# A hybrid layer stack on one core: ternary quantisation of the feed-forward weights moved beside the gated memory

## The chip, the cores and the metric

The kernel runs on one core of one Trainium2 chip. A core has five instruction queues that work beside each other and wait for each other through semaphores: TensorE (PE, matmuls), VectorE (DVE), ScalarE (ACT), GpSimd (POOL) and SyncE (SP, which here issues every DMA). The metric is the device time of the program in microseconds (us), as the median over runs. One execution was profiled; its trace gives a start and a duration for each instruction.

## The reference

Four sub-layers follow one another on a residual stream of 2048 tokens (2 sequences of 1024) by 512 features: a gated linear memory, a feed-forward, a differential attention, and the same feed-forward again with the same weights. Each takes a layer norm of the stream.

```python
x = x + gated_memory(layernorm(x), w_in, w_out)
x = x + ffn(layernorm(x), w_gate_up, w_proj)
x = x + differential_attention(layernorm(x), ...)
x = x + ffn(layernorm(x), w_gate_up, w_proj)
```

The gated memory projects to q, k, v, a, g, and per channel runs a recurrence in chunks of 64 tokens: `prefix = cumprod(a)`, `acc = cumsum(k*v / max(prefix, 1e-6))`, `states = prefix * (state + acc)`, then `y = gate*(q*states) + (1-gate)*v` and a last projection. The feed-forward is `rms_norm(silu(gate) * up) @ w_proj`, and both its weight matrices are first made ternary:

```python
w = w_fp32.astype(bfloat16); w_g = w.reshape(-1, 64)
scale = clip(mean(abs(w_g), axis=-1, keepdims=True), 1e-8, None)
q = clip(round(w_g / scale), -1, 1)
w_hat = (q * scale).reshape(w.shape)
return w + stop_gradient(w_hat - w)
```

So each group of 64 weights becomes -scale, 0 or +scale, and the difference to w is rounded once in bf16 before w is added back.

## The kernel before

**Stage A, the gated memory** (lines 138 to 289). The 2048 tokens are 4 blocks of 512 (`t`), and the 512 channels are 4 chunks of 128 (`c`), channels on the partitions and tokens along the free dimension. Per block, PE first makes the q projections, then for each chunk the k, v, a and g projections (`kv`, `ag`, in a PSUM pool of two slots) and a broadcast of the q norms (`pr`, in a PSUM pool of four banks). ACT evicts these with tanh, sigmoid or copy. DVE and POOL then pass one 128x512 chunk to and fro, in this order:

- POOL: `u*v` (L232)
- DVE: clip of a (L233), `qn` (L273), `a_start`, memset, the scan for `prefix` (L239), its maximum and reciprocal `inv` (L242, L243)
- POOL: `u*inv` (L244)
- DVE: the scan for `acc` (L246), the scan over chunk states (L253), `acc+state` (L262)
- POOL: `acc*prefix` (L268); DVE: `acc*qn` (L274); POOL: `acc-v` (L275); DVE: `acc*gate` (L276); POOL: `yt = acc+v` (L277)

When the four chunks of a block are in `yt`, PE projects them (`a_out`, L284: 4 tiles of 128 tokens by 4 chunks of channels, so 16 matmuls, each of which is recorded as two passes) and DVE adds them to the residual `xres` (L289). The next block's layer norm and transposes (`xn`, `xnt`, in `a_input`) are issued before that projection, and the q projections of the next block after it.

**The feed-forward** (L336 on) is called twice. A block of 512 tokens goes through 16 chunks `f` of the hidden dimension: gate and up projections (L370), `silu(gate)*up` split into a high and a low part `hs` on ACT and DVE (L375 to L379), the down projection into four PSUM banks (L391), one chunk behind. `finish_block` takes the mean square (`msq`), a square root on ACT (`inv`, L404) and adds to the residual (L408). The weights of all 16 chunks stay in SBUF as tiles `ws[f]` of 128 by 3 by 512 (gate, up, down), in pools that lie where those of stage A were.

In the first call (`with_quant`) the ternary weights are made during the first block of 512 tokens: `ternary_chunk(f+1)` is issued ahead of the matmuls of chunk f. `ternary` works on one 128x512 tile: a DMA, three ACT passes (bf16 copy, magnitude, sign), a matmul with `groupmean` that leaves each group's mean in all of its rows, and on DVE the eviction of the scale (L309), the comparison (L312), the products with sign and scale (L313, L314) and the difference to w (L316); POOL adds w (L318) and ACT casts into `ws[f]` (L319). Three tiles make a chunk, which is also written to a DRAM tile `w_kept[f]` (L329). The second call loads `ws[f]` from there (L418).

**What sets the order.** The text of the program is traced once, a scheduler places the instructions of each engine in one fixed list, and each engine works through its list in order. An instruction whose inputs are late holds up all behind it on its engine. Tile pools with two buffers make the writer of a tile wait for the readers of the tile two before.

Of the kernel before, what the change touches and what calls it, by code (L numbers as in the profile page):

```python
# [10 lines left out]
F32 = mybir.dt.float32  # L11
F32R = mybir.dt.float32r
# [5 lines left out]
P = 128  # L18
# [24 lines left out]
def kernel(  # L43
# [91 lines left out]
        return pt.rearrange("p (c t) -> p c t", c=NKC)  # L135


    with ExitStack() as s:
        open_psum(s, "a")
        wa = s.enter_context(tc.tile_pool(name="wa", bufs=1))  # L140
        ap_ = s.enter_context(tc.tile_pool(name="a_act", bufs=2))

        w_sec = []
        for i in range(5):
# [54 lines left out]
        for t in range(NBLK):  # L199

            q = ap_.tile([P, NKC, BLK], F32, tag="q", name=f"q{t}", bufs=1)
            pss = bank(f"pss{t}")
            for c in range(NKC):
                pq = bank(f"pq{t}_{c}")
                project(pq, w_q, c, xt)
                nc.scalar.copy(q[:, c, :], pq)
                sq = ap_.tile([P, BLK], F32, tag="sq", name=f"sq{t}_{c}")
                nc.scalar.square(sq, pq)
                nc.tensor.matmul(
                    pss[:16, :], headmean[:, c, :], sq, start=(c == 0), stop=(c == NKC - 1)  # L210
                )
            rq = ap_.tile([16, BLK], F32, tag="rq", name=f"rq{t}")
            nc.scalar.activation(rq, pss[:16, :], AF.Sqrt, bias=rms_eps[:16])
            nc.vector.reciprocal(rq, rq)

            yt = ap_.tile([P, NKC, BLK], F32, tag="yt", name=f"yt{t}", bufs=1)
            for c in range(NKC):
                n = f"{t}_{c}"
                kv, ag = big(f"kv{n}"), big(f"ag{n}")
                project(kv[:, 0, :], w_k, c, xt)  # L220
                project(kv[:, 1, :], w_v, c, xt)
                project(ag[:, 0, :], w_a, c, xt)
                project(ag[:, 1, :], w_g, c, xt)
                u = ap_.tile([P, BLK], F32, tag="u", name=f"u{n}")
                nc.scalar.activation(u, kv[:, 0, :], AF.Tanh)
                v = ap_.tile([P, BLK], F32, tag="v", name=f"v{n}")
                nc.scalar.copy(v, kv[:, 1, :])
                a = ap_.tile([P, BLK], F32, tag="a", name=f"a{n}")
                nc.scalar.activation(a, ag[:, 0, :], AF.Sigmoid, bias=two)
                gate = ap_.tile([P, BLK], F32, tag="gate", name=f"gate{n}")  # L230
                nc.scalar.activation(gate, ag[:, 1, :], AF.Sigmoid)
                nc.gpsimd.tensor_mul(u, u, v)  # L232
                nc.vector.tensor_scalar(a, a, A_MIN, A_MAX, ALU.max, ALU.min)  # L233

                start = a_start[c % 2]
                nc.vector.tensor_copy(start[:, 0:BLK:CHUNK], a[:, 0:BLK:CHUNK])
                nc.vector.memset(a[:, 0:BLK:CHUNK], 0.0)
                prefix = ap_.tile([P, BLK], F32, tag="prefix", name=f"prefix{n}")
                nc.vector.tensor_tensor_scan(prefix, a, start, 0.0, ALU.mult, ALU.add)  # L239

                inv = ap_.tile([P, BLK], F32, tag="inv", name=f"inv{n}")
                nc.vector.tensor_scalar(inv, prefix, PREFIX_MIN, None, ALU.max)  # L242
                nc.vector.reciprocal(inv, inv)  # L243
                nc.gpsimd.tensor_mul(u, u, inv)  # L244
                acc = ap_.tile([P, BLK], F32, tag="acc", name=f"acc{n}")
                nc.vector.tensor_tensor_scan(acc, goes_on, u, 0.0, ALU.mult, ALU.add)  # L246

                state = ap_.tile([P, CPB + 1], F32, tag=f"state{c}", name=f"state{n}")
                if t % (SEQ // BLK) == 0:
                    nc.vector.memset(state[:, 0:1], 0.0)  # L250
                else:
                    nc.vector.tensor_copy(state[:, 0:1], before[c][:, CPB : CPB + 1])
                nc.vector.tensor_tensor_scan(  # L253
                    state[:, 1 : CPB + 1],
                    acc[:, CHUNK - 1 : BLK : CHUNK],
                    prefix[:, CHUNK - 1 : BLK : CHUNK],
                    state[:, 0:1],
                    ALU.add,
                    ALU.mult,
                )  # L260
                before[c] = state
                nc.vector.tensor_tensor(  # L262
                    acc.rearrange("p (n i) -> p n i", i=CHUNK),
                    acc.rearrange("p (n i) -> p n i", i=CHUNK),
                    state[:, 0:CPB].unsqueeze(2).to_broadcast([P, CPB, CHUNK]),
                    ALU.add,
                )
                nc.gpsimd.tensor_mul(acc, acc, prefix)  # L268

                pr = bank(f"pr{n}")  # L270
                nc.tensor.matmul(pr, headrow[:, c, :], rq, start=True, stop=True)
                qn = ap_.tile([P, BLK], F32, tag="qn", name=f"qn{n}")
                nc.vector.tensor_mul(qn, pr, q[:, c, :])  # L273
                nc.vector.tensor_mul(acc, acc, qn)  # L274
                nc.gpsimd.tensor_sub(acc, acc, v)  # L275
                nc.vector.tensor_mul(acc, acc, gate)  # L276
                nc.gpsimd.tensor_add(yt[:, c, :], acc, v)  # L277

            if t + 1 < NBLK:
                xt = a_input(t + 1)  # L280
            for j in range(TPB):
                po = bank(f"a_out{t}_{j}")
                for k in range(NKC):
                    nc.tensor.matmul(  # L284
                        po, yt[:, k, ts(j, P)], w_out[:, k, :],
                        start=(k == 0), stop=(k == NKC - 1),
                    )
                xi = xres[t * TPB + j]
                nc.vector.tensor_add(xi, xi, po)  # L289

    kept = ctx.enter_context(tc.tile_pool(name="kept", bufs=1, space=bass.MemoryType.DRAM))
    w_kept = [kept.tile([P, 3, D], F32R, tag=f"wk{f}", name=f"w_kept{f}") for f in range(NF)]

    def ternary(pool, dst, src, name):

        w32 = pool.tile([P, D], F32, tag="w32", name=f"w32_{name}", bufs=3)
        nc.sync.dma_start(out=w32, in_=src)
        w16 = pool.tile([P, D], BF, tag="w16", name=f"w16_{name}")  # L300
        nc.scalar.copy(w16, w32)
        mag = pool.tile([P, D], BF, tag="mag", name=f"mag_{name}")
        nc.scalar.activation(mag, w32, AF.Abs)
        sign = pool.tile([P, D], BF, tag="sign", name=f"sign_{name}")
        nc.scalar.sign(sign, w16)
        pm = ring(f"pm_{name}")
        nc.tensor.matmul(pm, groupmean, mag, start=True, stop=True)
        scale = pool.tile([P, D], BF, tag="scale", name=f"scale_{name}")
        nc.vector.tensor_scalar(scale, pm, SCALE_MIN, None, ALU.max)  # L309

        q = pool.tile([P, D], BF, tag="q", name=f"q_{name}")
        nc.vector.scalar_tensor_tensor(q, scale, TERNARY_CUT, mag, ALU.mult, ALU.is_lt)  # L312
        nc.vector.tensor_mul(q, q, sign)  # L313
        nc.vector.tensor_mul(q, q, scale)  # L314

        nc.vector.tensor_sub(q, q, w16)  # L316
        wq = pool.tile([P, D], BF, tag="wq", name=f"wq_{name}")
        nc.gpsimd.tensor_add(wq, q, w16)  # L318
        nc.scalar.copy(dst, wq)  # L319

    def ternary_chunk(pool, f, w):

        for e, src in enumerate((
            w_gu[f].rearrange("p c n -> p (c n)"),
            w_gu[NF + f].rearrange("p c n -> p (c n)"),
            w_pt[ts(f, P), :],
        )):
            ternary(pool, w[:, e, :], src, f"{'gud'[e]}{f}")
        nc.sync.dma_start(out=w_kept[f].bitcast(F32), in_=w.bitcast(F32))  # L329

    rings = []

    def ring(name):
        return rings[-1].tile([P, BLK], F32, tag="ring", name=name)

    def feed_forward(which, with_quant, store):  # L336
        with ExitStack() as s:
            wqp = s.enter_context(tc.tile_pool(name=f"wq{which}", bufs=1))
            ws = [wqp.tile([P, 3, D], F32R, tag=f"w{f}", name=f"w{which}_{f}") for f in range(NF)]
# [71 lines left out]
                    if store:  # L411
                        nc.sync.dma_start(out=out[ts(i, P), :], in_=xres[i])

            if with_quant:
                ternary_chunk(fp, 0, ws[0])
            else:
                for f in range(NF):
                    nc.sync.dma_start(out=ws[f].bitcast(F32), in_=w_kept[f].bitcast(F32))  # L418
            xs = ff_input(0)
            waiting = []  # L420

# [6 lines left out]
            for t in range(NBLK):  # L428
# [3 lines left out]
                    for j in range(TPB)  # L432
                ]
                for f in range(NF):
                    if with_quant and t == 0 and f + 1 < NF:
                        ternary_chunk(fp, f + 1, ws[f + 1])
                    hp = gate_up(t, f, xs, ssq)
                    if waiting:
                        down_one()
# [5 lines left out]
                down_one()  # L445
            rings.pop()

    feed_forward(0, True, False)


    NQ = SEQ // P
# [434 lines left out]
            for j in range(e * QB, (e + 1) * QB):  # L886
                project_out(1, j, w_o)

    feed_forward(1, False, True)


_INS = [
# [57 lines left out]
```

## Time and profile before

| what | value |
|---|---|
| time of the program, median of 3 runs | 2530.82 us (2530.42 to 2536.12) |
| profiled execution: its own time, and the span of its trace | 2533.64 us, 2531.9 us |
| stage A: until the last addition of `a_out` | 419.1 us, four blocks of some 100 us |
| first block of the first feed-forward, to its `inv` | 419.1 to 632.8 us |
| second block of it | 632.8 to 725.9 us |
| first block of the second feed-forward, to its `inv` | 2141.0 to 2253.3 us |
| busy over the span: PE, DVE, ACT, POOL | 94%, 44%, 36%, 16% |

The stage times are starts of instructions in the trace: the last L289 of stage A, the last attention addition before the second feed-forward, and the L404 that ends a feed-forward block. A busy share is an average over stages with different limits; what a change in one stage is worth is read in that stage, from the wait that ends last there. Starts and durations in the trace overlap a little: the next instruction of an engine begins some 0.1 us before the recorded end of the one before, so costs are best taken from start to start.

### The profile page before, as it was taken

The page shows a single profiled execution, that of the slowest core. Times are in us where ns is not written, and L with a number is a line of the kernel's source. Part 1 is how long each engine was busy: PE and PEld are TensorE (multiplying, and loading weights), DVE is VectorE, ACT ScalarE, POOL GpSimd, SP SyncE. Part 2 cuts the span into 40 slices and gives each one's busy share as a digit, 9 for nine tenths or more (in the row PEclk, how much of TensorE's full clock was granted, in tenths as well). Part 3 has the DMA queues.
Part 4 walks back from the last instruction along what each step waited for, and adds up shares of the span by engine and source line. Part 5 has one row for each costly group of instructions (what it writes and reads, how often), then busy time and mean ns, then how long its engine had stood idle before and what let it go on. Part 6 is the DMA issues. An engine that isn't in the chain of part 4 may idle for free. (4 is left out here: it accounts for less than half of the span.)

```text
span 2531.9 us, 26379 instructions
## 1 busy us (share of the span) xinstructions
PE 2382.2 (94%) x10050; PEld 1362.7 (54%) x10128; DVE 1109.4 (44%) x1551; ACT 885.7 (35%) x1340; POOL 403.0 (16%) x555
## 2 busy tenths in 40 slices
PE   8999996667999989999999999999999997999998
PEld 3443432445787854444545444444444543787887
DVE  4653647887323243343434343333434434423322
ACT  2122122767333321343434341233434440333333
POOL 1321312344221210000000000100000001122122
PEclk9999997889999999999999999999999998999999
DMA  4000001333000024342333331133333301300000
GB/s 166 0 1 0 0 0 46 125 110 119 1 1 1 1 80 108 83 97 76 90 88 85 81 90 52 51 81 97 76 102 82 78 12 65 137 17 1 17 17 17
DMA packets 66350, 148.84 MB, mean 59 GB/s; under 512 B 16048, under 2 KB 24240, under 8 KB 66224
## 3 DMA queue, kind: packets, MB, share of 16 engines
q1 hardware_dynamic: 66224, 147.15, 20.3%
q8 instruction: 80, 1.31, 0.2%
q14 instruction: 46, 0.38, 0.0%
HBM read 96.50 MB, written 41.94 MB: 55 GB/s over the span
## 5 line engine op out<-in xcount | busy, mean ns | idle before, releaser
L715 ACT ACTIVATE pr<-t 128x1024 f32<-128x1024 f32 (+3 forms) x384 | 311.0, 812 | 498.8 <-PE t L713 351.0
L659 DVE TENSOR_REDUCE nmax<-s 128x1 f32<-128x640 f32 (+3 forms) x256 | 259.3, 1023 | 270.7 <-PE s L651 270.4
L730 PE MATMUL y<-pr,val 128*33 128x512 f32 (+3 forms) x1536 | 325.6, 493 | 0.0
L391 PE MATMUL f_out<-w,hs 128*128 128x512 f32 x1024 | 274.3, 409 | 30.1 <-ACT hs L378 29.0
L370 PE MATMUL g<-xs,w 128*128 128x512 f32 x1024 | 275.2, 412 | 0.7 <-ACT xs L359 0.7
L370 PE MATMUL u<-xs,w 128*128 128x512 f32 x1024 | 261.8, 397 | 0.0
L647 PE MATMUL s<-ks,qs 128*128 128x512 f32 (+3 forms) x768 | 256.9, 408 | 3.2 <-ACT lam L562 0.5
L385 POOL TENSOR_TENSOR ssq<-ssq,sq 128x512 f32<-128x512 f32 x120 | 157.8, 1315 | 558.6 <-ACT sq L384 558.6
L376 DVE TENSOR_TENSOR h<-h,u 128x512 f32<-128x512 f32 x128 | 88.0, 687 | 359.8 <-PE u L370 354.6
L391 PEld LDWEIGHTS f_out<-w,hs 128*128 128x128 f32 x1024 | 196.7, 194 | 88.3 <-ACT hs L378 38.8
L370 PEld LDWEIGHTS g<-xs,w 128*128 128x128 f32 x1024 | 200.1, 196 | 70.8 <-issue 16.0
L703 PE MATMUL t<-qs,ks 128*128 128x512 f32 (+3 forms) x768 | 237.7, 391 | 0.0
L370 PEld LDWEIGHTS u<-xs,w 128*128 128x128 f32 x1024 | 193.9, 189 | 47.6 <-ACT w L319 0.2
L703 PEld LDWEIGHTS t<-qs,ks 128*128 128x128 f32 x768 | 117.3, 192 | 122.0 <-DVE nmax L659 45.0
L674 POOL CAST maxima<-nmax 128x8 bf16<-128x8 f32 x64 | 12.9, 201 | 1049.4 <-DVE nmax L659 684.4
L707 PE MATMUL t<-mt_s,pick 128*128 128x512 bf16 (+3 forms) x690 | 174.3, 325 | 5.3
L573 PE MATMUL pq<-b_xt,w_qk 128*128 128x512 f32 x384 | 170.2, 597 | 0.0
L655 DVE TENSOR_REDUCE nmax<-s 128x2 f32<-128x256 f32 (+3 forms) x128 | 104.7, 824 | 130.2 <-PE s L651 96.9
L647 PEld LDWEIGHTS s<-ks,qs 128*128 128x128 f32 x768 | 132.4, 192 | 50.0 <-ACT pr L715 22.4
L378 ACT CAST hs<-h 128x512 fp32r<-128x512 f32 x128 | 79.3, 619 | 216.9 <-DVE h L376 216.9
L730 PEld LDWEIGHTS y<-pr,val 128*33 128x33 f32 x1536 | 78.6, 110 | 124.6 <-issue 95.6
L375 ACT ACTIVATE h<-g 128x512 f32<-128x512 f32 x128 | 76.4, 597 | 189.1 <-PE g L370 189.0
(178 smaller groups left out, 2701.5 us busy)
## 6 DMA issues: line engine op xcount, KB each, us to landing
qs<-sc SPq DMA_DIRECT2D x128, 256.0 KB, 4.4
sc<-parts SPq DMA_DIRECT2D x192, 128.0 KB, 2.2
ks<-sc SPq DMA_DIRECT2D x128, 128.0 KB, 3.6
w_kept<-w SPq DMA_DIRECT2D x16, 768.0 KB, 3.5
w<-w_kept SPq DMA_DIRECT2D x16, 768.0 KB, 14.2
share<-ys SPq DMA_DIRECT2D x128, 64.0 KB, 2.0
w_in<-in_w_in_t_dram SPq DMA_DIRECT2D x5, 1024.0 KB, 10.8
x<-in_x_dram SPq DMA_DIRECT2D x16, 256.0 KB, 7.1
```

What stands on the lines that cost most here:

```text
L370: nc.tensor.matmul(po, ws[f][:, part, ts(k, P)], xs[:, e, k, :], start=(k == 0 and e == 0), stop=(k == NKC - 1 and e == 1),)
L376: nc.vector.tensor_mul(h, h, pu)
L385: nc.gpsimd.tensor_add(ssq, ssq, sq)
L391: nc.tensor.matmul(po[j], hp[:, e, ts(j, P)], ws[f][:, 2, :], start=(f == 0 and e == 0), stop=(f == NF - 1 and e == 1),)
L573: nc.tensor.matmul(po[:, e, :], w[:, k, ts(kind, P)], xts[b][:, k, ts(e, BLK)], start=(k == 0), stop=(k == NKC - 1),)
L647: nc.tensor.matmul(dst, qs[:, ts(j, P)], ks[:, lo:hi], start=True, stop=not last)
L655: nc.vector.tensor_reduce(nmax[pair][:, j, :], po[:, :, :nk], AX.X, ALU.max, negate=True)
L659: nc.vector.tensor_reduce(nmax[pair][:, j, which : which + 1], po.rearrange("p e n -> p (e n)")[:, :nk], AX.X, ALU.max, negate=True,)
L703: nc.tensor.matmul(po[:, e, :nq], ks[:, ts(kb, P)], qs[:, q0 : q0 + nq], start=True, stop=False)
L707: nc.tensor.matmul(po[:, e, :nq], pick[:, e, :], turned[pair, qb][:, lo:], start=False, stop=not diagonal,)
L715: nc.scalar.activation(pr[:, :, :nq], po[:, :, :nq], AF.Exp)
L730: nc.tensor.matmul(y[64 * e : 64 * e + HV, lo:], val[:, kb, h, :], pr[:, e, : BLK - lo], start=(kb == 0), stop=last,)
```

## The change

The quantisation leaves the first feed-forward. `ternary_chunk` is rewritten to take all three tiles of a chunk at once, as one 128x3x512 tile, and is called at the end of each chunk of stage A: 4 blocks by 4 chunks, so once for each of the 16 weight chunks. It uses a new SBUF pool `ternary` with two buffers (`one` and `w` have one), and the PSUM pool of four banks that `pr`, the q projections, the transposes and `a_out` share. Both feed-forward calls then load `ws[f]` from `w_kept`.

The arithmetic is done on magnitudes: the magnitude is subtracted from the scale and added back (this gives the rounding of the difference in bf16), the result is multiplied by the comparison's 0 or 1 and last by the sign. The bf16 copy of w, two of the products and the cast on ACT go; the last product writes the wide format that the matmul reads. Of the wide operations DVE has the comparison, the subtraction and the last product, and POOL has the addition and the product with `one`.

```diff
+    def ternary_chunk(pool, f):
+
+        w32 = pool.tile([P, 3, D], F32, tag="w32", name=f"w32_{f}")
+        for e, src in enumerate((
+            w_gu[f].rearrange("p c n -> p (c n)"),
+            w_gu[NF + f].rearrange("p c n -> p (c n)"),
+            w_pt[ts(f, P), :],
+        )):
+            nc.sync.dma_start(out=w32[:, e, :], in_=src)
+        mag = pool.tile([P, 3, D], BF, tag="mag", name=f"mag{f}")
+        nc.scalar.activation(mag, w32, AF.Abs)
+        sign = pool.tile([P, 3, D], BF, tag="sign", name=f"sign{f}")
+        nc.scalar.sign(sign, w32)
+        scale = pool.tile([P, 3, D], BF, tag="scale", name=f"scale{f}")
+        for e in range(3):
+            pm = bank(f"pm{f}_{e}")
+            nc.tensor.matmul(pm, groupmean, mag[:, e, :], start=True, stop=True)
+            nc.vector.tensor_scalar(scale[:, e, :], pm, SCALE_MIN, None, ALU.max)
+
+        one = pool.tile([P, 3, D], BF, tag="one", name=f"one{f}", bufs=1)
+        nc.vector.scalar_tensor_tensor(one, scale, TERNARY_CUT, mag, ALU.mult, ALU.is_lt)
+
+        nc.vector.tensor_sub(scale, scale, mag)
+        nc.gpsimd.tensor_add(scale, scale, mag)
+        nc.gpsimd.tensor_mul(scale, scale, one)
+        w = pool.tile([P, 3, D], F32R, tag="w", name=f"w_made{f}", bufs=1)
+        nc.vector.tensor_mul(w, scale, sign)
+        nc.sync.dma_start(out=w_kept[f].bitcast(F32), in_=w.bitcast(F32))
...
+        tp = s.enter_context(tc.tile_pool(name="ternary", bufs=2))
...
                 nc.gpsimd.tensor_add(yt[:, c, :], acc, v)
+                ternary_chunk(tp, t * NKC + c)
...
-    def feed_forward(which, with_quant, store):
+    def feed_forward(which, store):
...
-            if with_quant:
-                ternary_chunk(fp, 0, ws[0])
-            else:
-                for f in range(NF):
-                    nc.sync.dma_start(out=ws[f].bitcast(F32), in_=w_kept[f].bitcast(F32))
+            for f in range(NF):
+                nc.sync.dma_start(out=ws[f].bitcast(F32), in_=w_kept[f].bitcast(F32))
...
-                    if with_quant and t == 0 and f + 1 < NF:
-                        ternary_chunk(fp, f + 1, ws[f + 1])
...
-    feed_forward(0, True, False)
+    feed_forward(0, False)
```

More of the change, by code (lines that the diff above doesn't have):

```diff
@@ L135, in normal_transposed @@
         return pt.rearrange("p (c t) -> p c t", c=NKC)
+    kept = ctx.enter_context(tc.tile_pool(name="kept", bufs=1, space=bass.MemoryType.DRAM))
+    w_kept = [kept.tile([P, 3, D], F32R, tag=f"wk{f}", name=f"w_kept{f}") for f in range(NF)]
+    def ternary_chunk(pool, f):
[23 more added lines that the diff above has]
+        nc.sync.dma_start(out=w_kept[f].bitcast(F32), in_=w.bitcast(F32))
     with ExitStack() as s:
@@ L289 @@
                 nc.vector.tensor_add(xi, xi, po)
[L293 to L329, printed above, removed]
     rings = []
@@ L887 @@
                 project_out(1, j, w_o)
-    feed_forward(1, False, True)
+    feed_forward(1, True)
 _INS = [
```

## The prediction

> **What bounds the kernel now.** I read the stretches of the trace first, then the waits of the first feed-forward, then DVE and POOL in order of time in one chunk of stage A. Busy time by stretch (columns: the stretch and its length, busy us and instructions of PE, its weight loads, DVE, ACT, POOL, the granted clock, DMA share, GB/s); the rows are the chunks of the last block of stage A, the first and second block of the first feed-forward, and the first block of the second feed-forward:
>
> ```profile
> 350.30:413.30 63.00, 56.72 (x128) 23.44 (x128) 43.15 (x48) 7.92 (x14) 24.16 (x19) 0.98 0.00 0
> 419.10:632.80 213.70, 142.24 (x491) 98.42 (x492) 182.31 (x329) 147.23 (x262) 81.04 (x63) 0.82 0.36 118
> 632.80:725.90 93.10, 92.33 (x410) 74.69 (x409) 30.11 (x45) 33.05 (x57) 19.36 (x15) 1.00 0.00 1
> 2141.00:2253.30 112.30, 102.87 (x444) 82.96 (x445) 46.24 (x89) 41.77 (x68) 19.34 (x15) 0.94 0.27 113
> ```
>
> The block that makes the ternary weights takes 213.7 us with DVE busy for 182.3; the same block of the second call, which loads them, takes 112.3 with DVE at 46.2. The longest waits between 419 and 633 us say the same: PE waits for `hs`, which stands in the queues of ACT and DVE behind the quantisation.
>
> ```profile
> PEld f_out L391 <- ACT hs L378: 38.8, 13, 6.4
> PE f_out L391 <- ACT hs L378: 29.0, 13, 6.1
> ```
>
> Stage A is less simple. PE has 15.0 us of matmuls per chunk (`a` of the last block is evicted at 350.29, 365.28, 380.26), but the DVE-POOL chain of a chunk takes 15.6, and each block ends with PE waiting for `yt` (2.15 us before L284 goes on at 214.04, 5.57 at 413.33). DVE, then POOL, in order of time:
>
> ```profile
> 366.13 0.42 DVE L233 TENSOR_SCALAR a<-a 128x512 f32<-128x512 f32 x1
> 366.47 0.69 DVE L273 TENSOR_TENSOR qn<-pr,q 128x512 f32<-128x512 f32 x1
> 367.07 0.64 DVE L236 COPY a_start<-a 128x8 f32<-128x8 f32 x1
> ...
> 369.60 3.35 DVE L243 RECIPROCAL inv<-inv 128x512 f32<-128x512 f32 x1
> 374.40 1.23 DVE L246 TENSOR_TENSOR_SCAN acc<-goes_on,u 128x512 f32<-128x512 f32 x1 [1.44 <-POOL u L244]
> ...
> 378.00 1.74 DVE L274 TENSOR_TENSOR acc<-acc,qn 128x512 f32<-128x512 f32 x1 [1.38 <-POOL acc L268]
> 381.11 0.69 DVE L276 TENSOR_TENSOR acc<-acc,gate 128x512 f32<-128x512 f32 x1 [1.38 <-POOL acc L275]
> 381.72 0.42 DVE L233 TENSOR_SCALAR a<-a 128x512 f32<-128x512 f32 x1
> ```
> ```profile
> 366.36 1.32 POOL L277 TENSOR_TENSOR yt<-acc,v 128x512 f32<-128x512 f32 x1 [0.87 <-PE pr L271]
> 373.10 1.26 POOL L244 TENSOR_TENSOR u<-u,inv 128x512 f32<-128x512 f32 x1 [5.42 <-DVE inv L243]
> 376.70 1.26 POOL L268 TENSOR_TENSOR acc<-acc,prefix 128x512 f32<-128x512 f32 x1 [2.34 <-DVE acc L262]
> 377.92 1.26 POOL L232 TENSOR_TENSOR u<-u,v 128x512 f32<-128x512 f32 x1
> ```
>
> L233 to L233 is 15.59 us. L274 takes 1.74 at 378.00 and 0.69 when POOL rests: POOL's `u*v` began at 377.92, and L274 ended 0.56 after POOL did. L273, with one input in PSUM, kept its 0.69 beside a POOL operation.
>
> **What the skill says.** The Trainium skill, "SBUF — State Buffer", Who interferes with whom: DVE and GpSimd share a port pair; a DVE instruction with two SBUF inputs, or a copy or tensor_scalar in a two-port mode, and a GpSimd instruction that reads SBUF exclude each other for a whole instruction, the first taking it. L274, and L236 beside L277, agree. Where POOL's next instruction follows at once, the trace shows the waiting one served first: DVE's L312 (463.85, 1.65 us) got in between a POOL L318 that ended at 464.96 and an L385 that came out at 1.71 instead of some 1.26.
>
> **Prices.** DVE from start to start: 0.34 for a float32 tensor_scalar in SBUF, 0.60 from PSUM or for a 512-wide two-input operation, 0.34 for a bf16 tensor_tensor (L316: 443.14, 443.48), 1.26 a scan, 3.4 the reciprocal. Twice the rate saves 0.26 per 512 elements, so 512 cost 0.53 and the fixed part is 0.07: 1536 wide are 1.67 at one per cycle (`one`; `w`, whose output is 32 bits) and 0.87 packed (`scale-mag`). "VectorE: DVE Perf Modes", The perf-mode tier table, has bf16 tensor_tensor at twice the rate, and L316 against L312 (0.42, 0.69 us) agrees. POOL: L318 takes 1.16 for 512 in bf16, so 1536 are at most 3.5; "GPSIMD Engine Reference", Elementwise — side-by-side cycle accounting, gives 4.50 us for 2048 float32, with L244's 1.26 for 512 a slope of 2.1 ns: 1.16+2.16=3.3. I take 3.4, an estimate.
>
> **Removed.** The first feed-forward becomes like the second: 213.7-112.3 = 101.4 us less. Its weight loads, the 16 reads of 768 KB, are inside the 112.3; the kept weights' writes move to stage A, where the DMA queues stand idle (share 0.00).
>
> **Added per chunk of stage A.** PE: three `pm`, under 2 us beside the 15.0, hidden by the wait for the chain. ACT: two wide passes (some 1.5 each: L303 takes 0.62 for a third), in front of the next `a`; they wait for `mag` and `sign` of two chunks before, which ends before DVE asks for `a`. SP: three loads and a write, two chunks ahead. DVE: 3x0.60+1.67+0.87+1.67 = 6.0; POOL: 2x3.4 = 6.8. None of these is hidden on DVE and POOL, because the built order of the changed program puts them inside the chain. In chunk 1 the POOL list reads: add back, times `one`, `u*v` of chunk 2, then `u*inv` of chunk 1, for which the `acc` scan waits; and on DVE the last product stands ahead of that scan.
>
> Chunk 1 step by step, zero at its `qn`: the previous `yt` holds the port 0.2-1.5, clip -1.85, evictions and scan -5.06, `one` -6.73, maximum -7.07, `scale-mag` -7.94, reciprocal -11.3. POOL: add back 8.05-11.45, times `one` -14.85, `u*v` -16.1. DVE's `w` has waited for the product and takes the port 16.1-17.77, POOL's `u*inv` -19.03, DVE's scans and `acc+state` -21.3, `acc*prefix` -22.64, `*qn` -23.3, the next clip -23.7, `-v` -24.96, `*gate` 25.6.
>
> Chunk 0: `u*v` of chunk 1 comes first (v ready at 9.2), `u*inv` ends at 12.6, add back runs -16.05 and holds off the scan, which ends at 17.3, times `one` -20.7 holds off state and `acc+state` (-21.6), `w` -23.25, `*prefix` -24.55, the rest 27.3. Chunk 2: `u*inv` -10.6, `u*v` -11.8, scan -13.1, subtraction -13.9, add back -17.45 holds off `acc+state` (-18.1), times `one` 19.45-22.85 holds off `*qn` (-23.45), `w` -25.1, `-v` -26.4, 27.0. Chunk 3 is like chunk 0 without that `u*v`, with four `xn` of the next block among it: 30.4 until `yt`; 28.4 in the last block.
>
> Sum of a block: 27.3+25.6+27.0+30.4 = 110.3, against 62.3 now (351.01 to 413.33). All of the 48.0 shows, as PE already waits for `yt`. Then `a_out`: in blocks 0 to 2 the built order has 12 matmuls behind the last `yt` where it had 4, so 8 x 0.86 = 7 us more. Together 3x48+46+3x7 = 211.
>
> **Sum against the profiled execution**: span 2531.9+211-101.4 = 2641.5, with 1.7 around it 2643; the median shown lies 2.8 below that execution, so 2640.
>
> **Bounds of the unknown.** `w` at the packed rate: -13. `scale-mag` unpacked: +13. The reciprocal holding the port against add back in chunk 1: +13. POOL's width: +-3. PE's clock falls when it waits (0.82 in the table's second row); some 2 us more per block after the longer waits: +8. The likeliest case's own range is 2610 to 2678.
>
> **Rivals.**
> 1. The port costs little: only the order counts. The same steps without exclusion give 22.9, 22.7, 22.0 and 23.2, so 90.8 per block: 4x28.5+21-101.4 = +34, 2564. Against it stand L274 and L312 above.
> 2. Faster: the chain overlaps across chunks, and a chunk costs what DVE is busy, 43.15/4+6.0 = 16.8, only 1.2 more than now: 16x1.2+21-101.4 = -61, 2470. For it: POOL is busy for 24 of 63 us, DVE for 43. It wins where a chunk grows by less than (101.4-21)/16 = 5.0 us. Against it: POOL's list has both wide operations, 6.8 us, in front of `u*inv` or between it and `acc*prefix`.
> 3. The move hides nothing in the first feed-forward: its weights arrive late. The second call issued its loads at 2141.07 and PE began on them at 2153.6, with a median landing of 14.2 us; if the last writes of `w_kept` delay them by their landing (3.5) and each of the first chunks waits, some +10: 2650, within the range.
>
> **Chances.** Forecast 0.74, rival 1 0.15, rival 2 0.07, rival 3 and worse 0.04. The range takes in rival 1: 2565 to 2678. Within 0.3% (2523 to 2538) is about what a measurement can't tell from no change: 0.02. Faster 0.07, slower 0.91.
>
> **What would show it.** Right: stage A ends near 630 us, POOL's two 1536-wide operations near 3.4 us each, DVE's `acc` scan or `acc+state` stretched to 3 us or more beside them, PE waiting some 45 us for `yt` per block, and the block after it near 112. Wrong: a chunk of 20 us or less, so that the exclusion or the order is not what I read; or POOL's wide operations near 2 us, which would take 16x2.8 = 45 us off.

## The result and the profile after

The changed kernel takes 2609.37 us (2607.54 to 2609.82) against 2531.86 (2530.42 to 2536.12): ratio 1.0302, with a 95% interval of 1.0284 to 1.032. The span of the profiled execution went from 2531.9 to 2607.4 us.

Busy time by stretch after (columns: the stretch and its length, busy us and instructions of PE, its weight loads, DVE, ACT, POOL, the granted clock, DMA share, GB/s). The rows are the four chunks of the last block of stage A, and the first block of the first feed-forward:

```profile
487.40:589.80 102.40, 62.67 (x139) 25.69 (x140) 81.00 (x72) 13.62 (x18) 58.82 (x27) 0.84 0.08 31
596.20:707.90 111.70, 102.29 (x444) 82.53 (x444) 46.19 (x89) 41.73 (x68) 19.38 (x15) 0.94 0.28 113
```

The feed-forward gained what it was meant to: its first block takes 111.7 us where it took 213.7, so 102.0 less. Stage A ends at 596.2 us instead of 419.1, so 177.1 more. The difference, 75.1, is all but 0.4 of the change of the span (75.5). In the first row the four chunks take 102.4 us instead of 63.0; DVE is busy for 38 us more and POOL for 35 more, and a chunk grew by 9.8 us where PE's work grew by 1.5. The sum 81.0+58.8 = 139.8 is more than the stretch, but this does not show that the two engines work side by side: as the lines below show, part of an instruction's recorded time can be time in which the other engine holds it off.

What PE waited for until 596 us (columns: the waiting engine, tile and line, the releaser, us in all, times, the longest):

```profile
PE xnt_a L134 <- DVE qn L308: 60.9, 3, 20.9
PE xnt_a L134 <- DVE state L288: 47.3, 3, 15.8
PE ag L228 <- ACT gate L266: 23.7, 8, 4.9
PE a_out L320 <- DVE qn L308: 20.7, 1, 20.7
PE a_out L320 <- POOL yt L312: 17.9, 4, 13.0
```

These waits end in DVE's and POOL's chain, the third by way of ACT, whose evictions are late. They add up to 170.5 us, 43 per block: PE finishes a block's projections and stands still until the chain has produced `yt`.

DVE and then POOL in chunk 0 of the third block after the change, in order of time (start, duration in us, engine, line; L281 is the `acc` scan, L288 the state scan, L297 `acc+state`, L168 the last product of the quantisation, L165 and L166 POOL's two wide operations, L303 `acc*prefix`; in brackets the idle time of the engine just before the instruction, and what ended it). The first fence is the state scan of one chunk before the change, for comparison:

```profile
375.66 0.24 DVE L253 TENSOR_TENSOR_SCAN state<-acc,state,prefix 128x8 f32<-128x8 f32 x1
```
```profile
348.07 3.35 DVE L278 RECIPROCAL inv<-inv 128x512 f32<-128x512 f32 x1
351.33 0.89 DVE L164 TENSOR_TENSOR scale<-scale,mag 128x1536 bf16<-128x1536 bf16 x1
354.60 4.09 DVE L281 TENSOR_TENSOR_SCAN acc<-goes_on,u 128x512 f32<-128x512 f32 x1 [2.37 <-POOL u L279]
358.73 2.88 DVE L288 TENSOR_TENSOR_SCAN state<-acc,state,prefix 128x8 f32<-128x8 f32 x1
361.64 0.69 DVE L297 TENSOR_TENSOR acc<-acc,state 128x512 f32<-128x512 f32 x1
362.31 1.75 DVE L168 TENSOR_TENSOR w_made<-scale,sign 128x1536 fp32r<-128x1536 bf16 x1
```
```profile
351.23 2.11 POOL L267 TENSOR_TENSOR u<-u,v 128x512 f32<-128x512 f32 x1 [14.27 <-ACT v L262]
353.31 1.26 POOL L279 TENSOR_TENSOR u<-u,inv 128x512 f32<-128x512 f32 x1
354.52 3.09 POOL L165 TENSOR_TENSOR scale<-scale,mag 128x1536 bf16<-128x1536 bf16 x1
357.69 3.88 POOL L166 TENSOR_TENSOR scale<-scale,one 128x1536 bf16<-128x1536 bf16 x1
362.41 2.78 POOL L303 TENSOR_TENSOR acc<-acc,prefix 128x512 f32<-128x512 f32 x1 [0.84 <-DVE state L287]
```

The scan L281 takes 1.22 us elsewhere and 4.09 here: POOL's L165 began first, at 354.52, and the scan ended 1.1 us after it. The scan over 8 states, 0.24 us before the change, takes 2.88, to the end of L166. L166 in turn is recorded with 3.88 instead of 3.08: the scan L281 went ahead of it, to 358.69, and L166 needed the rest. L303 waits for L168 in the same way. From the start of L165 to the end of L166 the chain advances by one scan of 1.2 us and the short one that ends with L166.

### The profile page after: what moved, and what is told of

It is laid out like the page before. It is cut to its first block, busy times and chain, and to the rows that moved or that the text cites. A ratio compares the mean times of both kernels' runs of the same rounds, so it can differ in the third digit from the quotient of the medians.

```text
span 2607.4 us, 25965 instructions
## 1 busy us (share of the span) xinstructions
PE 2366.9 (91%) x10046; PEld 1356.1 (52%) x10128; DVE 1127.9 (43%) x1407; ACT 825.9 (32%) x1178; POOL 476.3 (18%) x539
## 3 DMA queue, kind: packets, MB, share of 16 engines
q1 hardware_dynamic: 68528, 159.73, 20.5%
## 5 line engine op out<-in xcount | busy, mean ns | idle before, releaser
L367 PE MATMUL g<-xs,w 128*128 128x512 f32 x1024 | 263.8, 399 | 1.4 <-ACT xs L356 1.4
L388 PE MATMUL f_out<-w,hs 128*128 128x512 f32 x1024 | 261.3, 395 | 0.0
L367 PEld LDWEIGHTS g<-xs,w 128*128 128x128 f32 x1024 | 193.7, 190 | 47.8 <-ACT xs L356 2.2
```

The source lines that it names most:

```text
L367: nc.tensor.matmul(po, ws[f][:, part, ts(k, P)], xs[:, e, k, :], start=(k == 0 and e == 0), stop=(k == NKC - 1 and e == 1),)
L388: nc.tensor.matmul(po[j], hp[:, e, ts(j, P)], ws[f][:, 2, :], start=(f == 0 and e == 0), stop=(f == NF - 1 and e == 1),)
```

## The experiments

Each run is compared with the kernel before on the same chip; a ratio above 1 is slower than that kernel.

| run | quantisation stands | wide adds and products on | us | ratio (95% interval) |
|---|---|---|---|---|
| changed kernel | inside each chunk | POOL | 2609.4 | 1.0302 (1.0284 to 1.0320) |
| dma_only | left out of stage A | none | 2433.6 | 0.9604 (0.9589 to 0.9618) |
| no_pool_wide | inside each chunk | left out | 2533.0 | 0.9997 (0.9989 to 1.0006) |
| dve_wide | inside each chunk | DVE | 2549.6 | 1.0060 (1.0043 to 1.0077) |
| pool_in_thirds | inside each chunk | POOL, 512 wide | 2610.6 | 1.0307 (1.0291 to 1.0322) |
| moved_only | inside each chunk, old arithmetic | as before | 2573.8 | 1.0162 (1.0145 to 1.0179) |
| rewritten_in_place | in the feed-forward | POOL, 768 wide | 2568.4 | 1.0134 (1.0119 to 1.0149) |
| rewritten_dve | in the feed-forward | DVE | 2537.0 | 1.0017 (1.0010 to 1.0024) |
| moved_early | start of each block | POOL | 2527.0 | 0.9969 (0.9958 to 0.9980) |
| moved_early_dve | start of each block | DVE | 2463.9 | 0.9726 (0.9711 to 0.9740) |
| moved_ahead_dve | before a_out of the block before | DVE | 2473.1 | 0.9763 (0.9748 to 0.9777) |

### What of stage A's loss is quantisation: dma_only

```diff
-        mag = ...   # down to the product with `one`: all of it
         w = pool.tile([P, 3, D], F32R, tag="w", name=f"w_made{f}", bufs=1)
-        nc.vector.tensor_mul(w, scale, sign)
+        nc.scalar.copy(w, w32)
```

> The quantisation is left out of stage A: the three loads and the write of each chunk stay, and between them only one ACT pass copies the weights, so the feed-forwards work with unquantised weights. Theory (DVE's and POOL's added work stands in the chain, nothing else costs): stage A is back at 419 us, a block's period near 100.4, a_out has 4 matmuls behind the last yt again, and only the feed-forward's gain is left: 2531.9-102 = 2430 (2424 to 2440). Rival (the loads, the write or the ACT passes in front of the next chunk's evictions cost as well): stage A stays above 440 and the time above 2450.

Measured 2433.6, 98 below the kernel before. Stage A ends at 422.1 us (419.1 before), a block's period is 102 (100.4). The loads, the write and one ACT pass cost some 3 us; all the rest of the 177 comes with the quantisation itself, its work on DVE, POOL and PE and the other of its two ACT passes. So some 98 us are to be had, if the quantisation can be hidden altogether.

### What POOL's two wide operations cost: no_pool_wide, dve_wide

```diff
-        nc.gpsimd.tensor_add(scale, scale, mag)
-        nc.gpsimd.tensor_mul(scale, scale, one)
```

> POOL's two 1536-wide operations are left out of the changed kernel, so the weights written are (scale-magnitude) times sign and wrong; all of DVE's, ACT's and PE's work stays. Theory (both POOL operations and the waits at the shared port are in series with the chain): a chunk is 15.6 plus evictions 1.8, comparison 1.67 and product 1.67, the subtraction hidden behind u*inv: 20.7 against 25.4 now, so a block from a_0 to yt 83 instead of 104, and 2609-83 = 2526 (2510 to 2540). Rival (DVE's added 6 us is what counts, POOL runs mostly beside it): a chunk loses 2 us or less, 2577 or more.

```diff
-        nc.gpsimd.tensor_add(scale, scale, mag)
-        nc.gpsimd.tensor_mul(scale, scale, one)
+        nc.vector.tensor_add(scale, scale, mag)
+        nc.vector.tensor_mul(scale, scale, one)
```

> The two wide operations (add back, times one) run on DVE instead of POOL, 0.87 us each in packed bf16; everything is computed. Theory (POOL's 3.08 us each and the port are what lengthens the chain): a chunk is 20.7+2x0.87 = 22.5, a block from a_0 to yt 90, and 2609-4x13.6 = 2554 (2535 to 2570), slower than the kernel before still. Rival (DVE is the bound of a chunk, so what it takes over adds to the time): 16x1.74 = 28 more, 2637.

Without the two operations the time falls by 76 us to 2533.0, a chunk (`yt` to `yt`, second block) takes 20.6, 20.2 and 20.5 us; the theory said 20.7 and 2526. So they cost 4.8 us per chunk of the 6.2 that they last. With them on DVE the chunks take 21.6, 20.1 and 19.9 us and the time is 2549.6, not the rival's 2637: the two packed operations (0.86 us each from start to start) add next to nothing to these chunks, since the built order of this run also puts the next chunk's clip, `qn` and first eviction into the gaps at the end of the chain. Some 9 us of the 16.6 by which dve_wide is slower than no_pool_wide lie between the blocks: `a_out` runs for 15.5 us in a row from 264.17 (11.4 from 259.35 in no_pool_wide), and from the start of the last `yt` to the next `a` it is 47.0, 47.9 and 48.4 us instead of 44.9; the first chunk of each block, up to its `yt`, is 1.4 to 1.6 us longer, some 6 in all. Either way, DVE's own quantisation in the chain eats up what the feed-forward gains.

### Whether it is the shared port or one long instruction: pool_in_thirds

```diff
-        nc.gpsimd.tensor_add(scale, scale, mag)
-        nc.gpsimd.tensor_mul(scale, scale, one)
+        for e in range(3):
+            nc.gpsimd.tensor_add(scale[:, e, :], scale[:, e, :], mag[:, e, :])
+        for e in range(3):
+            nc.gpsimd.tensor_mul(scale[:, e, :], scale[:, e, :], one[:, e, :])
```

> Each of POOL's two 1536-wide operations is issued as three of 512, 1.16 us each (7.0 us of POOL a chunk instead of 6.2); the built order now has u*inv ahead of the add back in every chunk, and acc*prefix behind the first third of the product. Theory (DVE and POOL exclude each other one instruction at a time, so POOL's and DVE's SBUF work still add up, in turns): stepping through a chunk gives 25.2, so 2609 as before (2590 to 2625). Rival (no exclusion, or only while one long instruction holds the port): 21.6 a chunk, 2609-16x3.8 = 2548.

Measured 2610.6; the chunks take 25.4, 25.4 and 25.9 us in the second block, against a theory of 25.2 and a rival of 21.6. DVE and then POOL in order of time in chunk 1 of the third block (here L283 is the `acc` scan, L290 the state scan, L299 `acc+state`, L311 `acc*qn`, L170 the last product; L166 and L168 are the thirds):

```profile
381.86 2.16 DVE L283 TENSOR_TENSOR_SCAN acc<-goes_on,u 128x512 f32<-128x512 f32 x1 [1.15 <-POOL u L281]
384.05 0.94 DVE L290 TENSOR_TENSOR_SCAN state<-acc,state,prefix 128x8 f32<-128x8 f32 x1
385.02 1.59 DVE L299 TENSOR_TENSOR acc<-acc,state 128x512 f32<-128x512 f32 x1
388.88 1.62 DVE L311 TENSOR_TENSOR acc<-acc,qn 128x512 f32<-128x512 f32 x1 [2.20 <-POOL acc L305]
```
```profile
381.79 4.28 POOL L166 TENSOR_TENSOR scale<-scale,mag 128x512 bf16<-128x512 bf16 x3
386.03 1.60 POOL L168 TENSOR_TENSOR scale<-scale,one 128x512 bf16<-128x512 bf16 x1
388.81 2.70 POOL L168 TENSOR_TENSOR scale<-scale,one 128x512 bf16<-128x512 bf16 x2
```

Every one of DVE's four operations is 0.7 to 0.95 us longer than when it is alone, by the rest of a 512-wide POOL operation, and POOL's three take 4.28 instead of 3.5. That agrees with the Trainium skill, "SBUF — State Buffer", Who interferes with whom: the two engines exclude each other for a whole instruction. This run adds that cutting the instruction changes the length of a turn and not the sum.

### The move without the rewriting: moved_only

```diff
+    def ternary_chunk(pool, f):
+        w = pool.tile([P, 3, D], F32R, tag="w", name=f"w_made{f}", bufs=1)
+        for e, src in enumerate(...):
+            ternary(pool, w[:, e, :], src, f"{'gud'[e]}{f}")   # the kernel before's, with pm in the bank pool
...
                 nc.gpsimd.tensor_add(yt[:, c, :], acc, v)
+                ternary_chunk(tp, t * NKC + c)
```

> The move without the rewriting: the kernel before's own arithmetic, tile by tile, called at the end of each chunk of stage A as in the changed kernel (DVE 6.9 us a chunk in 512-wide operations, POOL one addition of 1.16 us per tile, 3.5 a chunk instead of 6.2, four ACT passes); both feed-forwards load. Everything is computed. Theory (what stands in the chain is what DVE and POOL add up to, whatever the arithmetic): a chunk is 15.6 plus some 5.9 of DVE plus two of the three POOL additions, 2.3, so 23.8, and 2609-16x1.6 = 2583 (2555 to 2610), slower than the kernel before by some 2%. Rival (the wide operations on POOL alone turn a good move into a bad one; with the short ones the move pays): 2532 or less.

Measured 2573.8, within the range; chunks of 23.1, 22.7 and 22.2 us. So the move alone costs 41 us, and the rewriting another 36: on POOL it has 6.2 us a chunk where the old arithmetic had one addition per tile, 3.5. DVE's 6.9 us of old arithmetic against the 6.0 of the new made up for little of that. dve_wide, which has the rewriting but nothing of it on POOL, is 24 us faster than this run, so it is POOL's share that makes the rewriting slower here.

### The rewriting without the move: rewritten_in_place, rewritten_dve

```diff
+        for hf in range(2):
+            cols = ts(hf, D // 2)
...
+            nc.gpsimd.tensor_add(scale, scale, mag)      # nc.vector in rewritten_dve
+            nc.gpsimd.tensor_mul(scale, scale, one)      # nc.vector in rewritten_dve
+            nc.vector.tensor_mul(w[:, :, cols], scale, sign)
```

> The kernel before, with only the rewriting: the quantisation stays in the first feed-forward, works on three tiles at once on magnitudes, in two halves of 128x768[...], with the two wide operations on POOL. Everything is computed. Theory (the move, not the rewriting, is what costs): what DVE and POOL do on the shared port per chunk, 5.0+7.5 = 12.5 us, is the pace instead of 13.4 now, so the first block is some 200 us instead of 213.7 and the time 2518 (2490 to 2535). Rival (the rewritten arithmetic is itself no cheaper wherever it stands): 2532 or more.

> As the run with the rewriting alone in the first feed-forward, with add back and times one on DVE instead of POOL. Everything is computed. Theory: DVE's 8.3 us per chunk of quantisation and 2.9 of its own are the pace, 11.2, so 16x11.2 = 179 us for the block and 2531.9-34.5 = 2497 (2475 to 2515). Rival (DVE is the bound, so taking over POOL's work makes it slower than the version with POOL): above that version's time.

Both forecasts were too fast by 40 to 50 us: 2568.4 and 2537.0. With POOL the first block ends at 666.6 instead of 632.8. The longest waits in it (columns as above):

```profile
POOL scale L320 <- DVE scale L319: 110.3, 32, 15.3
ACT sign L311 <- DVE w L322: 65.6, 28, 3.8
DVE w L322 <- POOL scale L321: 63.6, 30, 2.8
```

DVE waits for POOL in nearly each of the 32 halves, and POOL for DVE: in DVE's list the last product of a half stands ahead of the comparison and the subtraction of the next, so the two engines take turns by dependence, not only at the port. My sum had counted their work, 12.5 us, and no round trips; a chunk took 14.1 (541.38 to 555.48, from one last product to the next but one). The halves double those round trips, so this run says less on the rewriting with whole chunks. On DVE the block ends at 635.3 (632.8 before): DVE is busy for 193.4 of the 218 us from 422 to 640, with `hs` at a mean of 1.61 us instead of some 0.8 in the same block of the kernel before. It is stretched beside POOL's `ssq` additions (1.75 us at 530.74, with POOL's L379 from 530.41 to 531.94), which the sum had left out. These 15 stretched operations are some 12 of the 40 us; the rest was not taken apart. In this place neither form of the new arithmetic gains anything.

### The same work at another place: moved_early, moved_early_dve, moved_ahead_dve

```diff
         for t in range(NBLK):
+            for c in range(NKC):
+                ternary_chunk(tp, t * NKC + c)
             q = ap_.tile([P, NKC, BLK], F32, tag="q", name=f"q{t}", bufs=1)
...
                 nc.gpsimd.tensor_add(yt[:, c, :], acc, v)
-                ternary_chunk(tp, t * NKC + c)
```

> The changed kernel, with the four chunks of quantisation of a block called at the block's start, ahead of the q projections, instead of one at the end of each chunk; POOL keeps its two wide operations. Everything is computed. Theory (the same work costs less where PE has 36 us of a_out, q and first projections while DVE and POOL wait, but DVE and POOL still exclude each other there, 4.2+6.2 = 10.4 us per quantised chunk, 42 per block): a block's period is some 116 us, the first block loses some 30, and the time is 2510 (2485 to 2540), some 100 below the changed kernel. Rival (without exclusion DVE's 6.0 and POOL's 6.2 run beside each other, 25 per block): 2450 or less, and below the version with all of it on DVE.

> As the run with the four chunks called at the block's start, with add back and times one on DVE instead of POOL. Everything is computed. Theory: 7.74 us per quantised chunk, 31 per block, of which most lies beside PE's a_out, q and first projections: a block's period is some 106 instead of 100.4, the first block loses some 25, and the time is 2470 (2445 to 2500), faster than the kernel before by 2 to 3%. Rival (what is moved out of the chunks comes back as late first chunks, one for one): 2550, as with all of it on DVE inside the chunks.

With nothing but this move of the call, the loss of 3% becomes a gain of 0.3%: 2527.0, inside the range. With the two wide operations on DVE as well it is 2463.9, 2.7% faster than the kernel before and 145 us faster than the changed one. Busy time of the third block and of most of the first block of the first feed-forward in moved_early_dve (columns as above; the second row begins 5.3 us after the last addition of stage A, from which the block takes 111.8 us):

```profile
257.90:363.50 105.60, 98.77 (x236) 40.78 (x236) 81.23 (x92) 31.56 (x42) 25.54 (x20) 0.98 0.14 53
455.90:562.40 106.50, 102.37 (x444) 82.56 (x445) 40.92 (x76) 40.19 (x67) 19.35 (x15) 0.95 0.25 104
```

DVE is busy for 81 us of the block, against 88 of 146 us in the third block of the changed kernel (341.41 to 487.41, time held off by POOL included), but here PE is busy for 98.8 of 105.6: `a_out`, the q projections and the first k, v, a, g projections run beside the quantisation, and the chunks then keep their old 15.6 us. The last addition of stage A is at 450.6, 31.5 us later than before instead of 177, and 31.5-102 is the -70 of the span (2461.6).

In moved_early a block lasts 121.3 us (297.11 to 418.45, `a` to `a`), 5 more than expected, and stage A ends at 514.9. DVE and POOL while they quantise (L162 is the comparison, L164 the subtraction, L168 the last product):

```profile
400.62 0.94 DVE L164 TENSOR_TENSOR scale<-scale,mag 128x1536 bf16<-128x1536 bf16 x1
407.93 2.81 DVE L168 TENSOR_TENSOR w_made<-scale,sign 128x1536 fp32r<-128x1536 bf16 x1 [5.77 <-POOL scale L166]
410.66 1.75 DVE L162 SCALAR_TENSOR_TENSOR one<-scale,mag 128x1536 bf16<-128x1536 bf16 x1
412.93 0.94 DVE L164 TENSOR_TENSOR scale<-scale,mag 128x1536 bf16<-128x1536 bf16 x1
```
```profile
401.64 3.09 POOL L165 TENSOR_TENSOR scale<-scale,mag 128x1536 bf16<-128x1536 bf16 x1 [10.94 <-DVE scale L164]
404.81 3.10 POOL L166 TENSOR_TENSOR scale<-scale,one 128x1536 bf16<-128x1536 bf16 x1
413.95 3.08 POOL L165 TENSOR_TENSOR scale<-scale,mag 128x1536 bf16<-128x1536 bf16 x1 [4.83 <-DVE scale L164]
```

This chunk takes 12.3 us from L165 to L165 (the next 11.3), against some 8.5 on DVE alone. That is more than my 10.4 for the port: DVE stands idle for 5.77 us before L168, and POOL for 4.83 before the next L165. So here the round trip between the two engines costs more than the port, which shows in these lines only in L168 (2.81 us instead of 1.75, behind a POOL `u*v`).

```diff
             if t + 1 < NBLK:
                 xt = a_input(t + 1)
+            if t + 1 < NBLK:
+                for c in range(NKC):
+                    ternary_chunk(tp, (t + 1) * NKC + c)
             for j in range(TPB):
                 po = bank(f"a_out{t}_{j}")
```

> As the run with the chunks called at the block's start and everything on DVE, but called one step earlier: those of block t+1 between its layer norm and the a_out of block t (those of block 0 still at its start). Everything is computed. Theory (DVE then starts on them while PE still waits for the last yt, and PE does the first projections of the next block ahead of a_out): PE's own work, 95 us a block, becomes the bound, a block's period is some 97 instead of 106, three times, and the time is 2440 (2425 to 2460). Rival (the earlier quantisation only delays the last chunk of the block by what it saves later): 2464 as in that run, or more.

The edit is shown in part: the chunks of block 0 are called ahead of the loop over the blocks, the call at the end of each chunk is gone, and the two wide operations are on DVE. Missed: 2473.1, the rival's side. A block's period is 109 us (291.33 to 400.34, from `a` to `a` of the second chunk) instead of 105.4. The first chunk of quantisation now stands in the last chunk of the block, which takes 20.5 us (218.94 to 239.47) instead of 15.8 from `yt` to `yt`; and PE reaches `a_out` only at 252.89, though `yt` was there at 241.4, because the groups' means of all four chunks and the first projections stand ahead of it in its list. What DVE starts earlier, PE pays back.

## Why the prediction was right, and where its sum was off

The direction, the mechanism and its place were right: forecast 2640 (own range from 2610), measured 2609.4, just below that range and well inside the wide one. In the profiled span the forecast was 2641.5 and the measurement 2607.4, 34 us less. The errors of any size all go the same way, so the agreement does not come from errors that cancelled; but the measurement lies at the very edge of the own range. Point by point:

- **Removed**: 101.4 forecast, 102.0 measured. No wait for late weights: PE's first gate matmul ran at 608.82, 12.6 us after the loads were issued, as in the second call. Rival 3 did not occur.
- **Hidden work**: the loads, the write and one ACT pass cost some 3 us in dma_only. PE's three `pm` are hidden in the chunk, as forecast: PE waits 43 us per block.
- **The chunk**: the order of events is the one stepped through. Lengths forecast 27.3, 25.6, 27.0 and 30.4; measured in the third block 25.8, 24.4, 25.2 and 27.1, so 7.8 us less per block. In chunk 1, POOL's two operations took 0.32 us less each (3.08 for an estimated 3.4), DVE's work up to the subtraction 7.57 instead of 7.94, and the rest 0.2 less. In chunk 3 an `xn` stood waiting beside POOL's product (3.24 us), where the forecast had added four of them in full.
- **POOL's wide operations** are the largest single term that was mis-sized: 16x2x0.32 = 10 of the 34 us, where the bound had said 3 either way. The slope of 2.1 ns per element was float32's; bf16's is (3.08-1.16)/1024 = 1.9.
- **The base**: the 62.3 us per block were those of the last block, without the `xn` of a next one; the second block took 63.6 (150.4 to 214.04). That takes 1.3 us from the growth of three blocks, 4 in all.
- **The 12 matmuls of `a_out`**: 24 recorded passes from 444.70 to 455.10, 10.4 us, where the forecast had 12x0.86. From their start to the next `a` (487.41) it is 42.7 us against 35.8 before (214.04 to 249.88), 6.9 more for a forecast of 7.
- **The sum**: 3x(7.8+1.3)+6.0 in the last block (40.0 measured for 46)+0.6 in the feed-forward = 33.9 of the 34.1.
- **Rival 1** (the port costs little, 2564) missed by 45 us, and pool_in_thirds, for which 2548 was expected without exclusion, took 2610.6. What moved_early adds is that the port is not the only reason why DVE and POOL add up: where one waits for the other's result in a fixed list, they alternate even without it. How the 4.8 us per chunk of POOL's wide operations divide between the two was not measured; no run here has POOL's work without the port.
- **Rival 2** (the chain overlaps, a chunk costs what DVE is busy) named a break-even of 5.0 us a chunk. no_pool_wide, with 4.8 us less than the changed kernel, grew by about 5 and ended at 0.9997 of the kernel before: that point was right.
- **The bounds**: the product to 32 bits ran unpacked (1.67 us from start to start, in moved_early_dve at 273.73), the subtraction packed (0.87). That shows the packed rate better than the prediction's L316 against L312, which are two different operations. And the reciprocal was not held by add back (3.34 at 375.47, with POOL's L165 at 375.62). Of the 8 us for PE's clock (0.84 in the last block's chunks, 0.98 before) hardly anything came: `a_out` took 10.4 us for 10.3 forecast, and from its restart to the last addition of stage A it is 6.4 us instead of 5.8.

What I did not see is how much the place of the call decides. The prediction found DVE and POOL idle on average, and the chain bound, but did not ask what the same instructions would cost at the start of the block.

## What to carry to other kernels

Work moved "beside" a stage is beside it only if the idle engine is not in the chain that ends the stage; here DVE and POOL were idle between the steps of a chain that PE already waited for, and the free time lay a few instructions earlier, beside `a_out` and the q projections, where the same work cost 96 us of stage A instead of 177, and 31 with the two wide operations on DVE. Whether the old arithmetic would gain as much at that place was not run. Before splitting elementwise work between DVE and POOL, add both engines' work and the round trips between them: two packed operations of 0.87 us on DVE were cheaper than two of 3.08 on POOL inside the chunks and at the block's start, and so were their halves in the feed-forward. And try a move and a rewriting apart: here each alone, in its first form, made the kernel slower, and another placement of the rewritten work made it faster.

## What the runs showed of the hardware

- POOL's two-input bf16 operation takes 1.16 us for 512 elements (before), 1.64 for 768 (rewritten_in_place) and 3.08 for 1536 (changed kernel): 0.2 us plus 1.9 ns per element.
- Scans with two SBUF inputs are held off by POOL like other such DVE operations, however short they are: in the changed kernel the one over 8 elements took 2.88 us instead of 0.24. The reciprocal, with one input, ran beside POOL undisturbed (3.34 us at 375.47, 3.35 before).
- When POOL has two operations in a row and a DVE operation waits, that one came between where this was looked at: in the changed kernel L166 was recorded with 3.88 us instead of 3.08 where the `acc` scan went ahead of it.
